# A four-layer image network: first loads on three queues, two output stages in source order, and first images read back in slices

## The chip, the cores and the metric

The kernel runs on one core of a Trainium2 chip. The metric is the device time of one execution in microseconds (us). All data are fp32. The engines are named as in the profile: PE is TensorE (matrix products and transposes), with PEld its weight loads; DVE is VectorE; ACT is ScalarE; POOL is GpSimd; SP is SyncE, which only issues DMAs. POOL and ACT can issue DMAs too.

## The reference

The input is x, 8 images of 56 x 56 positions with 192 channels. Four residual layers follow one another, each of the form x = x + f(GN(x)), where GN is a group normalisation over 32 groups of an image.

```
x = x + L0(_gn(x))    # silu projections, Toeplitz mixing along rows and columns, projection
x = x + L1(_gn(x))    # LN, shifted 7x7 window attention, 6 heads, projection
x = x + L2(_gn(x))    # 192 -> 384, 3x3 depthwise conv, four EMA scans, LN, 384 -> 192
x = x + L3(_gn(x))    # 7x7 depthwise conv + bias, LN, 192 -> 768, gelu, 768 -> 192, scale
return x
```

Layer 2's scans run s = 0.6 s + 0.4 x along rows and columns in both directions; their mean is added to the convolution's result before the layer norm (LN) over 384 channels. Layer 3's LN is over 192 channels.

## The kernel before

The layers run one after another over all 8 images, and most stages hand their results on through DRAM. On PE the stages lie at these times of the profiled execution: layer 0's projections 34 to 868 (L366), layer 0's mixing 875 to 2097; layer 1 2098 to 3558; layer 2's input projection (L790) 3613 to 3857; layer 2's mixing (L834, L858) 3885 to 4490; layer 2's output with layer 3's input (L911, L926, L973) 4546 to 5050; layer 3's convolution (L1009) 5072 to 5372; layer 3's output (L1065, L1087, L1098) 5411 to 6343.

**Order.** The program is written in Python with a tile framework. A scheduler decides the order of the instructions on every engine from dependences and priorities; tile pools with a number of buffers (`bufs`) make an instruction wait until the buffer that it needs is free, and tiles of different pools can lie on the same bytes, so a load into a new stage's tile can wait for the last reader of an old stage's tile. Each engine then works through its own list in order. DMAs are issued in the order of the list of the engine that issues them.

**Layer 1's start.** `layer1_load` (L595) loads an image rolled by 3 rows and columns, with 18 DMAs (`rolled`, L585), all on SP. `loaded` (L1165) loads images 0 and 1 before layer 0's mixing ends. The last store of layer 0's result is L476; `layer1_norm` begins at L600 with ACT's normalisation (L614) and PE's means (L621). At an image's end `rolled(x2[b], x[b], True)` stores it with 18 DMAs.

**Layer 2's input.** `layer2_in` (L765) loads an image on SP with two DMAs, normalises it on DVE (L778), clears borders on POOL (L776, L781), projects it on PE (L790), adds the bias on DVE and stores the tile pt to pd. The weights w_in and b_in are loaded by POOL's queue.

**Layer 2's mixing.** `layer2_mix` (L801) goes over 24 groups of 16 channels. `load` brings the band matrix wt and zc, the group's channels of all 8 images, 8 DMAs on SP. `front` (L828) convolves on PE (L834), copies loc and rows on ACT (L843), adds on POOL (L847), scans on DVE (L849 onwards); `back` (L854) multiplies by ema (L858) and copies to yc on ACT (L869); 8 DMAs per group store yc to md (L885). loc, rows and sums are one tile per group, of which `front` fills a quarter at a time.

**Layer 2's output and layer 3's input.** `layer2_load` (L888) loads one image of md as ml (112 partitions x 384 channels x 28 positions, 4.8 MB). `ln_pieces` (L187) takes bn_stats of the 28 pieces on DVE (L189); `ln_var` (L191) and `ln_rows` (L206) turn them into scale and shift with small DVE operations and one square root on ACT. An image has four groups k of up to four row pairs. `layer2_norm` (L893) scales ml into yt on DVE (L905) and ACT (L907), transposes it on PE (L911) and copies it to y with ACT (L912). `layer2_out` (L918) does the projection po on PE (L926) and adds it into x2o on DVE (L931), for three channel blocks j. After each block `between` (L1266) lets through an eighth of the next image's statistics and one or two steps of `layer3_in` (L935) of the image before: group statistics (L143 to L181), the normalised zp on POOL (L952), PE transposes zps (L973), copies zt (L960, L962) and the store zd (L986).

**Layer 3.** `convolve` (L988) goes over 12 groups of 16 channels like layer 2's mixing: wt (L997), zc (L1002), PE products cps (L1009), copies yc, 8 stores to yd per group (L1023). Then `layer3_load` (L1025) loads an image of yd as yl (2.75 MB), `layer3_norm` (L1035) adds the bias on POOL in four parts (L1043), takes 28 bn_stats (L189), computes rows, scales into yt on DVE (L1058), transposes on PE (L1065) and copies to y on ACT (L1076). `layer3_out` (L1078) does the two products ph (L1087) and po (L1098) with gelu into hid on ACT between (L1091), adds on DVE (L1105), and calls `between()` after every second ph block, twelve times an image, to let through one step of the next image's norm. yl has two buffers, and image b + 2 is loaded at the start of image b.

Of the kernel before, what the change touches and what calls it, by code (L numbers as in the profile page):

```python
# [29 lines left out]
HEADS, HD, WN = 6, 32, 49  # L30
C2 = 384
# [3 lines left out]
NPAIR = H // 2  # L35
# [41 lines left out]
def kernel(ctx: ExitStack, tc: tile.TileContext, a: dict, out: bass.AP):  # L77
# [113 lines left out]
    def ln_var(st, P, nch, pool):  # L191

        mean = pool.tile([P, NPAIR], F32, name="ln_mean")
        nc.vector.tensor_tensor(mean, st[:, :, 1], st[:, :, 4], ALU.add)
        d = pool.tile([P, NPAIR], F32, name="ln_d")
        nc.vector.tensor_tensor(d, st[:, :, 1], st[:, :, 4], ALU.subtract)
        nc.vector.tensor_tensor(d, d, d, ALU.mult)
        var = pool.tile([P, NPAIR], F32, name="ln_var")  # L200
        nc.vector.tensor_tensor(var, st[:, :, 2], st[:, :, 5], ALU.add)
        nc.vector.tensor_scalar(var, var, 1.0 / nch, None, ALU.mult)
        nc.vector.scalar_tensor_tensor(var, d, 0.25, var, ALU.mult, ALU.add)
        return mean, var

    def ln_rows(mean, var, P, eps, pool):  # L206

        rs = pool.tile([P, NPAIR], F32, name="ln_rs")
        nc.scalar.activation(rs, var, AF.Sqrt, bias=eps[0:P])
        nc.vector.reciprocal(rs, rs)  # L210
        mr = pool.tile([P, NPAIR], F32, name="ln_mr")
        nc.vector.scalar_tensor_tensor(mr, mean, -0.5, rs, ALU.mult, ALU.mult)
        return rs, mr

# [370 lines left out]
    def rolled(dram_image, tile_image, store):  # L585

        d = dram_image.rearrange("(j p) (h w) -> p j h w", p=64, w=W)
        for s, h0, h1, r0 in ((0, 0, 28, 3), (1, 0, 25, 31), (1, 25, 28, 0)):
            for w0, w1, c0 in ((0, 53, 3), (53, 56, 0)):
                for j in range(3):  # L590
                    sb = tile_image[64 * s:64 * s + 64, j, h0:h1, w0:w1]
                    dr = d[:, j, r0:r0 + h1 - h0, c0:c0 + w1 - w0]
                    nc.sync.dma_start(dr, sb) if store else nc.sync.dma_start(sb, dr)

    def layer1_load(b, pool):  # L595
        x = pool.tile([128, 3, H // 2, W], F32, name="x1")
        rolled(x1[b], x, False)
# [167 lines left out]
    def layer2_in(b, pool, xpool, psum, w_in, b_in):  # L765

# [5 lines left out]
        nc.sync.dma_start(x[0:64, :, 1:R2], src[:, :, 0:R2 - 1])  # L772
        nc.sync.dma_start(x[64:128, :, 0:R2 - 3], src[:, :, R2 - 1:H])
# [27 lines left out]
    def layer2_mix():  # L801
# [5 lines left out]
        with ExitStack() as st:  # L807
# [9 lines left out]
            def load(g):  # L817
# [5 lines left out]
                zc = pool.tile([128, nimg, CG2, P2], F32, name="zc2")  # L823
                for b in range(nimg):
                    nc.sync.dma_start(zc[:, b], pd[b][:, cs])
                return wt, zc

            def front(c4, wt, zc, loc, rows, sums):  # L828
# [9 lines left out]
                loc, rows, sums = (z[:, c4:c4 + 4].rearrange("p c z -> p (c z)") for z in (loc, rows, sums))  # L838
# [13 lines left out]
                )  # L852

            def back(c4, yc, loc, rows, sums):  # L854
                ps = psum.tile([2 * W, 2, 512], F32, name="mx2")
                for i in range(2):
                    for k, z in enumerate((loc, sums)):
                        nc.tensor.matmul(  # L858
                            ps[:, i, 0:2 * NG], ema[:, k],
                            z[:, c4 + 2 * i:c4 + 2 * i + 2].rearrange("p c z -> p (c z)"),  # L860
# [12 lines left out]
            for g in range(n + 1):  # L873
# [3 lines left out]
                following = [pool.tile([128, CG2, NG], F32, name=z) for z in ("loc", "rows", "sums")] if g < n else None  # L877
                for c4 in range(0, CG2, 4):
                    if g:
                        back(c4, yc, *now)  # L880
                    if g < n:
                        front(c4, *loaded[g], *following)
                if g:
                    for b in range(nimg):
                        nc.sync.dma_start(md[b][:, (g - 1) * CG2:g * CG2], yc[:, b])  # L885
                now = following

    def layer2_load(b, pool):  # L888
        ml = pool.tile([2 * W, C2, NPAIR], F32, name="ml")
        nc.sync.dma_start(ml, md[b])  # L890
        return ml, pool.tile([2 * W, NPAIR, 6], F32, name="ln_st")

    def layer2_norm(k, ml, rs, mr, pool, psum):  # L893


        n0 = 4 * k
        nn = min(4, PH - n0)
        nt = 2 * W * nn
        y = pool.tile([128, 3, 2, 8 * W], F32, name="y2")
        for s in range(2):  # L900
            yt = pool.tile([2 * W, 4, C2], F32, name="yt2")
            for i in range(nn):
                n = PH * s + n0 + i
                if i % 2 == 0:
                    nc.vector.tensor_scalar(yt[:, i], ml[:, :, n], rs[:, n:n + 1], mr[:, n:n + 1], ALU.mult, ALU.add)  # L905
                else:
                    nc.scalar.activation(yt[:, i], ml[:, :, n], AF.Identity, bias=mr[:, n:n + 1], scale=rs[:, n:n + 1])  # L907
            for m in range(3):
                tp = psum.tile([128, 4, 2 * W], F32, name="tp2")
                for i in range(nn):  # L910
                    nc.tensor.transpose(tp[:, i], yt[:, i, 128 * m:128 * m + 128], ident[0:2 * W, 0:2 * W])  # L911
                nc.scalar.activation(  # L912
                    y[:, m, s, 0:nt], tp[:, 0:nn].rearrange("p i n -> p (i n)"), AF.Identity,
                    bias=vec("be2", m), scale=vec("g2", m),
                )
        return y

    def layer2_out(k, y, x, psum, w_out, between):  # L918
# [3 lines left out]
        for j in range(3):  # L922
            ps = psum.tile([128, 512], F32, name="po2")
            for m in range(3):
                for s in range(2):
                    nc.tensor.matmul(  # L926
                        ps[64 * s:64 * s + 64, 0:nt], w_out[:, m, 64 * j:64 * j + 64], y[:, m, s, 0:nt],
                        start=(m == 0), stop=(m == 2),
                    )
# [489 lines left out]
```

## Time and profile before

| what | us |
|---|---|
| median of 3 runs | 6330.82 (6327.23 to 6345.44) |
| the profiled execution's own time | 6351.08 |
| its span, first to last instruction | 6349.2 |
| PE busy | 5569.1 (88% of the span) |
| DVE, ACT, POOL busy | 3439.3, 2239.7, 1302.1 |
| mean granted PE clock | 0.914 of full speed |

The profile is of one execution. Busy time of an engine says how long it had an instruction in work; a stage's bound shows in the stretch that holds it, in what ended the idle time of the engine that was idle. A row of waits reads: engine, operation and line that waited, after the arrow what ended the wait, then total us, times, and the longest. In a row of a stretch, behind its length, stand busy us and the number of instructions of each engine, the granted PE clock (which falls when PE is idle), the DMA engines' share and GB/s. In the chain each row has start, length and what ran. "issue" is time in which the profile shows no wait.

### The profile page before, as it was taken

How to read it: one execution, taken by the hardware profiler on the slowest of the kernel's cores; microseconds unless marked ns; L12 is line 12 of the kernel's file. 1: busy time of each engine (PE TensorE's matmuls, PEld its weight loads, DVE VectorE, ACT ScalarE, POOL GpSimd, SP SyncE). 2: the span in 40 equal slices, each digit the busy share in tenths (PEclk: the TensorE clock that was granted, in tenths of full speed). 3: DMA queues.
4: the chain of work that ended last, by engine and by line, in shares of the span. 5: the costliest groups of instructions: out<-in, count | busy, mean ns of one | idle time of the engine just before them, and what ended most of it. 6: DMA issues, size and time to landing. Idle time of an engine off the chain costs nothing. (4 is left out here: it accounts for less than half of the span.)

```text
span 6349.2 us, 126376 instructions
## 1 busy us (share of the span) xinstructions
PE 5569.1 (88%) x55636; PEld 3587.9 (57%) x55636; DVE 3439.3 (54%) x4752; ACT 2239.7 (35%) x2922; POOL 1302.1 (21%) x813
## 2 busy tenths in 40 slices
PE   6799989999999688888888598999588798789999
PEld 5677766666666345545445375777244498344444
DVE  5677765555665344444444486888688511532321
ACT  2334444443344233333332102555355300333333
POOL 1100034544444122122121102333110100110100
PEclk8899999999999888888888799999798799899999
DMA  6799886666665613444433675666667488121211
GB/s 166 185 221 210 188 262 263 260 253 240 240 252 194 88 33 55 60 58 63 55 48 44 103 266 208 224 228 233 153 203 208 170 305 305 64 67 56 70 54 27
DMA packets 1039131, 1013.10 MB, mean 160 GB/s; under 512 B 832104, under 2 KB 964372, under 8 KB 1011572
## 3 DMA queue, kind: packets, MB, share of 16 engines
q1 hardware_dynamic: 1028064, 954.17, 53.7%
q0 software_dynamic: 5648, 31.32, 1.5%
q10 hardware_dynamic: 4868, 19.52, 0.9%
q8 instruction: 437, 7.16, 0.5%
q14 instruction: 114, 0.93, 0.0%
HBM read 676.28 MB, written 345.08 MB: 161 GB/s over the span
## 5 line engine op out<-in xcount | busy, mean ns | idle before, releaser
L366 PE MATMUL qv<-w_qv_sb,xn 64*112 64x288 f32 x5376 | 722.2, 425 | 50.9 <-DVE act L372 47.6
L404 POOL COPY lc<-lt 128x896 f32<-128x896 f32 (+1 forms) x320 | 573.0, 1808 | 616.7 <-PE op L412 598.7
L366 PEld LDWEIGHTS qv<-w_qv_sb,xn 64*112 64x112 f32 x5376 | 535.5, 184 | 232.8 <-DVE act L372 64.7
L1087 PE MATMUL ph<-y,w_sb 64*128 64x392 f32 x2304 | 429.9, 511 | 49.1 <-ACT hid L1091 49.1
L373 ACT ACTIVATE act<-act 112x576 f32<-112x576 f32 x448 | 299.5, 682 | 461.7 <-DVE act L372 428.2
L1098 PE MATMUL po<-hid,w_sb 128*64 128x392 f32 x2304 | 395.1, 496 | 10.8 <-ACT hid L1091 10.8
L412 PEld LDWEIGHTS op<-rc,lc 128*56 128x56 f32 x9216 | 308.4, 136 | 127.6 <-issue 65.7
L412 PE MATMUL op<-rc,lc 128*56 128x56 f32 x9216 | 339.7, 222 | 46.0 <-POOL lc L404 24.2
L424 PE MATMUL pj<-xn,w_p_sb 64*128 64x392 f32 (+1 forms) x1920 | 373.0, 515 | 7.7 <-issue 4.7
L445 PE MATMUL y<-pp,w_o_sb 128*64 128x392 f32 (+1 forms) x1920 | 355.9, 503 | 20.4 <-DVE x L453 11.6
L372 DVE TENSOR_TENSOR act<-qv,b_qv 112x576 f32<-112x576 f32 x448 | 320.8, 751 | 86.1 <-PE qv L366 85.7
L1105 DVE TENSOR_TENSOR x<-x,z 128x392 f32<-128x392 f32 x96 | 55.8, 581 | 557.9 <-ACT z L1103 557.9
L1087 PEld LDWEIGHTS ph<-y,w_sb 64*128 64x128 f32 x2304 | 230.5, 194 | 224.1 <-ACT hid L1091 55.2
L404 ACT COPY rc<-rt 128x896 f32<-128x896 f32 (+1 forms) x160 | 256.9, 1606 | 230.7 <-PE op L412 216.0
L834 PE MATMUL cv<-zc,wt 128*128 128x224 f32 x1536 | 312.8, 355 | 27.9 <-DMA zc<-pd 27.9
L834 PEld LDWEIGHTS cv<-zc,wt 128*128 128x128 f32 x1536 | 290.5, 189 | 71.0 <-issue 54.9
L705 POOL TENSOR_TENSOR e<-e,mx 128x1176 f32<-128x1176 f32 x64 | 139.9, 2186 | 925.1 <-DVE mx L704 874.4
L655 PE MATMUL qk_ps<-xr,wg 64*96 64x392 f32 x1536 | 309.6, 511 | 14.9 <-ACT qk L661 13.3
L438 DVE TENSOR_TENSOR pp<-pp,ot 128x784 f32<-128x784 f32 (+1 forms) x160 | 154.6, 967 | 308.4 <-ACT pp L429 287.2
L1009 PE MATMUL cps<-zc,wt 128*128 128x224 f32 x1536 | 299.3, 356 | 23.1 <-DMA zc<-zd 22.5
L1009 PEld LDWEIGHTS cps<-zc,wt 128*128 128x128 f32 x1536 | 290.0, 189 | 32.5 <-issue 24.9
L847 POOL TENSOR_TENSOR rows<-rows,loc 128x896 f32<-128x896 f32 x96 | 228.1, 2377 | 390.2 <-ACT rows L843 262.8
(206 smaller groups left out, 9321.5 us busy)
## 6 DMA issues: line engine op xcount, KB each, us to landing
lt<-left SPq DMA_DIRECT2D x72, 1792.0 KB
rt<-right SPq DMA_DIRECT2D x72, 1792.0 KB
left<-qv SPq DMA_DIRECT2D x224, 252.0 KB
right<-qv SPq DMA_DIRECT2D x448, 126.0 KB
wt<-in_band_dram SPq DMA_DIRECT2D x24, 2048.0 KB
wt<-in_band_dram SPq DMA_DIRECT2D x12, 4096.0 KB
pd<-pt SPq DMA_DIRECT2D x8, 5568.0 KB
zc<-pd SPq DMA_DIRECT2D x192, 232.0 KB
```

The lines of the kernel that those rows point to most:

```text
L366: nc.tensor.matmul(ps[s][:, which, 0:D1 // 2], xn[64 * s:64 * s + 64, j, bass.ts(i, 2 * W)], w_qv[64 * s:64 * s + 64, j, which, ns], start ...
L372: nc.vector.tensor_tensor(act, ps[s][:, :, 0:D1 // 2], b_qv[:, :, ns], ALU.add)
L373: nc.scalar.activation(act, act, AF.Silu)
L404: copy(c[:, 0:nu], raw.rearrange("p (w u d) -> p u d w", u=nu, d=64 // nu)[:, :, d0:d0 + 8])
L412: nc.tensor.matmul(op[64 * u:64 * u + W, i, :], lc[:, u, i], rc[:, u, i], start=True, stop=True)
L424: nc.tensor.matmul(ps[0:M, s, 0:TT], w_p[64 * s:64 * s + 64, j, d0:d0 + M], xn[64 * s:64 * s + 64, j, ts], start=(j == 0), stop=(j == 2),)
L445: nc.tensor.matmul(y[64 * s:64 * s + 64], w_o[0:M, c, 64 * j:64 * j + 64], pp[0:M, s], start=(c == gated[0][0]), stop=(c == gated[-1][0]),)
L655: nc.tensor.matmul(ps[s], wg[64 * s:64 * s + 64, j, c0:c0 + HC], xw[64 * s:64 * s + 64, j, gs], start=(j == 0), stop=(j == 2),)
L834: nc.tensor.matmul(dst, wt[:, c4 + i, 128 * q:128 * q + 128], zc[:, :, c4 + i, q:q + NPAIR], start=(q == 0), stop=(q == 1),)
L1009: nc.tensor.matmul(dst.rearrange("p (b n) -> p b n", n=NPAIR), wt[:, c4 + i, q * OP:(q + 1) * OP], zc[:, :, c4 + i, q:q + NPAIR], start=(q ...
L1087: nc.tensor.matmul(ps[:, s, 0:TT], w0[64 * s:64 * s + 64, j, m * 128:(m + 1) * 128], y[64 * s:64 * s + 64, j, ts], start=(j == 0), stop=(j ...
L1098: nc.tensor.matmul(ps[64 * s:64 * s + 64], w1[:, m, 64 * j:64 * j + 64], hid[:, m, s], start=(m == 0), stop=(m == 5),)
```

## The change

- `rolled` and `layer1_load` take a list of queues. Image 0 of layer 1 is loaded over SP, POOL and ACT in turn; image 1's load is written after image 0's normalisation. One unused x1 tile shifts which buffer image 0 gets.
- `layer2_image` is split from `layer2_in`: image 0 of layer 2 is loaded by POOL's queue, later ones by SP, each written ahead of the image before it. w_in and b_in go to ACT's queue.
- In both convolutions, the first group's eight zc loads are spread over SP, POOL and ACT.
- In layer 2's mixing, loc, rows and sums become tiles of a quarter group with 6, 3 and 6 buffers. After each group's stores POOL reads image 0's slice of md back into ml. `convolve` does the same for yd, and POOL adds the bias to the slice.
- Image 0 of both output stages has its statistics, rows and scaling per group of rows (8 pieces at a time), not for the whole image at first.
- Layer 2's output with layer 3's input, and layer 3's output, are put under `manual_schedule` for PE, ACT and DVE: these three engines run the instructions of the stage in the order in which the source writes them. The source order is written so that yt of the next group comes before, and its transposes after, the projection of a block; the next image's statistics lie in blocks 3 to 8 of 12. The next x2o load is written at group 0, before at group 2.
- In layer 3's output the next image's norm is spread over more steps: bias at once, five of statistics, one of rows, then scaling a step ahead of its transposes.

```diff
-    def ln_var(st, P, nch, pool):
+    def ln_var(st, nch, pool):
...
+                    eng = queues[j % len(queues)]
...
-                    nc.sync.dma_start(dr, sb) if store else nc.sync.dma_start(sb, dr)
+                    eng.dma_start(dr, sb) if store else eng.dma_start(sb, dr)
...
-            x.extend(layer1_load(b, xpool) for b in range(min(2, nimg)))
+            for _ in range(-nimg % 3):
+                xpool.tile([128, 3, H // 2, W], F32, name="x1")
+            x.append(layer1_load(0, xpool, (nc.sync, nc.gpsimd, nc.scalar)))
...
         for _ in steps:
             pass
+        if nimg > 1:
+            x.append(layer1_load(1, xpool))
...
-        w_in = resident("w_in", nc.gpsimd, pool)
-        b_in = resident("b_in", nc.gpsimd, pool)
+        x = [layer2_image(0, xpool, nc.gpsimd)]
+        w_in = resident("w_in", nc.scalar, pool)
+        b_in = resident("b_in", nc.scalar, pool)
         for b in range(nimg):
-            layer2_in(b, pool, xpool, psum, w_in, b_in)
+            if b + 1 < nimg:
+                x.append(layer2_image(b + 1, xpool, nc.sync))
+            layer2_in(b, x[b], pool, psum, w_in, b_in)
...
+                queues = (nc.sync,) if g else (nc.sync, nc.gpsimd, nc.scalar)
                 for b in range(nimg):
-                    nc.sync.dma_start(zc[:, b], pd[b][:, cs])
+                    queues[b % len(queues)].dma_start(zc[:, b], pd[b][:, cs])
...
                     for b in range(nimg):
                         nc.sync.dma_start(md[b][:, (g - 1) * CG2:g * CG2], yc[:, b])
+                    nc.gpsimd.dma_start(first[:, (g - 1) * CG2:g * CG2], md[0][:, (g - 1) * CG2:g * CG2])
...
                 for b in range(nimg):
                     nc.sync.dma_start(yd[b][:, cs], yc[:, b])
+                nc.gpsimd.dma_start(first[:, cs], yd[0][:, cs])
+                add_bias(first[:, cs], dwb[:, cs])
...
+        st.enter_context(tc.manual_schedule(engines=IN_ORDER))
+        stat = lambda: pool.tile([2 * W, NPAIR, 6], F32, name="ln_st")
+        rows, own, steps, ready, y = [None], stat(), iter(()), None, None
...
+        def scaled(b, k, s):
+
+            if b:
+                return layer2_scaled(k, s, ml[b], *rows[0], 4 * k, pool)
+            if s == 0:
+                ns = slice(4 * k, min(4 * k + 4, PH))
+                ln_pieces(own, ml[0], [PH * r + n for r in range(2) for n in range(ns.start, ns.stop)])
+                rows[0] = ln_rows(*ln_var(in_halves(own)[:, :, ns], C2, pool), eps5, pool)
+            return layer2_scaled(k, s, ml[0], *rows[0], 0, pool)
...
+            for j in range(3):
+                if after and j < 2:
+                    if after[0] and after[1] == 0 and j == 0:
+                        rows[0] = ln_rows(*var_next, eps5, pool)
+                    following = scaled(*after, j)
+                if n >= 0:
+                    layer2_out(k, j, y, x[b], psum, w_out)
+                    i = 3 * k + j
+                    if b + 1 < nimg and 3 <= i < 9:
+                        ln_pieces(st_next, ml[b + 1], range(NPAIR * (i - 3) // 6, NPAIR * (i - 2) // 6))
+                    if b + 1 < nimg and i == 8:
+                        var_next = ln_var(in_halves(st_next), C2, pool)
+                    for _ in range(1 if i < 5 else 2):
+                        next(steps, None)
+                if after and j < 2:
+                    layer2_turned(after[1], j, following, y_next, psum)
...
-        steps = layer3_norm(yl[0], pool, psum, dwb)
-        y = [next(steps)]
-        for _ in steps:
-            pass
+        if nimg > 1:
+            yl.append(layer3_load(1, lpool))
+        st.enter_context(tc.manual_schedule(engines=IN_ORDER))
+        own, steps = layer3_norm(yl[0], pool, psum, None), iter(())
+        y = [next(own)]
+
+        next(own), next(own), next(own)
+
+        def between():
+            next(own, None)
+            next(steps, None)
```

## The prediction

> **What bounds the kernel now.** I read the shares of the page first, then busy time by stage, then the waits, then the chain of waits.
>
> ```profile
> span 6349.2 us, 126376 instructions
> ...
> PE 5569.1 (88%) x55636; PEld 3587.9 (57%) x55636; DVE 3439.3 (54%) x4752; ACT 2239.7 (35%) x2922; POOL 1302.1 (21%) x813
> ```
>
> TensorE is busy for 88% of the span, so a gain can only come from its idle time, or from an order that feeds it better. The view of stretches shows where it is idle; I cut at its own gaps.
>
> ```profile
> core 0: us, PE busy (x) PEld busy (x) DVE busy (x) ACT busy (x) POOL busy (x), PEclk, DMA share, GB/s
> 3557.00:3614.00 57.00, 1.35 (x6) 0.50 (x4) 5.51 (x9) 0.00 (x0) 4.16 (x10) 0.54 1.04 128
> 3856.00:3885.00 29.00, 1.11 (x3) 0.50 (x2) 1.09 (x2) 0.00 (x0) 3.97 (x3) 0.54 0.96 357
> 3884.00:4491.00 607.00, 598.07 (x2304) 422.61 (x2304) 525.56 (x288) 303.60 (x383) 228.14 (x96) 0.99 0.64 213
> 4490.00:4547.00 57.00, 1.16 (x5) 0.57 (x4) 24.60 (x40) 2.40 (x4) 6.04 (x6) 0.53 0.95 222
> 4546.00:5050.00 504.00, 426.70 (x2408) 226.04 (x2408) 387.38 (x699) 271.80 (x390) 47.99 (x68) 0.89 0.61 179
> 5049.00:5073.00 24.00, 1.52 (x6) 1.07 (x5) 1.24 (x2) 0.88 (x2) 0.00 (x0) 0.50 0.92 332
> 5371.00:5418.00 47.00, 5.52 (x20) 3.04 (x19) 28.45 (x55) 2.92 (x5) 20.56 (x8) 0.53 0.64 259
> 5418.00:6342.00 924.00, 864.18 (x4930) 431.21 (x4929) 268.40 (x554) 316.89 (x402) 63.83 (x24) 0.95 0.17 54
> ```
>
> Five stage boundaries leave TensorE empty: 57, 29, 57, 24 and 47 us; a sixth, into layer 1, is 22.01 us after 2105.04. At the first, second and fourth the DMA engines are over 90% busy throughout. At the third and fifth it is VectorE that works (24.60 and 28.45 us). The waits name the releasers:
>
> ```profile
> DVE yt L1058 <- PE tp L1065: 79.7, 22, 5.3
> PE tp L911 <- DVE yt L905: 57.8, 4, 55.8
> PE pin L790 <- POOL xn L781: 55.6, 1, 55.6
> DVE xn L778 <- DMA x<-x: 50.3, 1, 50.3
> PE ph L1087 <- ACT hid L1091: 49.1, 6, 10.0
> DVE x2o L931 <- PE po L926: 48.3, 54, 4.4
> ```
>
> The last two are steady losses, inside layer 3's and layer 2's output. The chain at the fifth boundary is a whole-image load, then POOL's bias, then the statistics of all 28 pieces:
>
> ```profile
> 5377.29 9.97 DMA yl<-yd
> ...
> 5387.51 2.54 POOL yl L1043
> ...
> 5390.07 11.63 DVE ln_st L189 x28
> ...
> 5401.73 1.28 DVE ln_mean L196
> 5403.00 2.63 DVE ln_d L198
> 5405.64 2.49 DVE ln_var L201
> ...
> 5410.16 4.31 DVE yt L1058 x9
> ```
>
> **What the Trainium skill says.** "DMA: Bandwidth & Descriptors", Issuing engines are not separate DMA queues: all issuing engines feed the same 16 DMA engines, so more queues save issue time only. The trace agrees: at the first two boundaries above the DMA share is 1.04 and 0.96 from one queue. The same page, Latency and other measured facts, gives about 2 us as a DMA's fixed cost; here a small store of the mixed output, issued at 4103.62, landed at about 4106.3. "GPSIMD Engine Reference", 1. Specifications: POOL shares its SBUF interfaces with VectorE and contends with VectorE instructions of two SBUF inputs. The trace agrees: the L196, L198, L201 row sums cost 1.28 to 2.63 us while POOL adds the bias, and 0.1 to 0.2 us at 5571, where POOL is idle.
>
> **The change, part by part.** Signs: minus is time gained.
>
> *Layer 1's first loads.* Before, SyncE issues 36 small-packet loads (both first images) from 2058.78 to 2112, and only then the last store of layer 0, which lands at 2126; ScalarE's first layer-1 operation starts at 2126.21, though image 0 has been in since 2086. What ends last is the store. In the changed program's order SyncE issues 6 loads of image 0, then 20 of later images, then the store: 26 ahead of it in place of 36, so 10 x about 1.5 us of issue, but those loads were limited by the DMA engines (22 us an image), and the 12 loads moved off still run. I take -4. ScalarE's six loads stand before the last five layer-0 activations, and could hold them: +14 at worst, -5 at best.
>
> *Layer 2's first image.* Image 0's load goes to POOL's queue, without the 18 last stores of layer 1 before it (3555.74 to 3594). But in the new order of VectorE, the first normalisation of image 1 stands before those of image 0, and image 1's load is on SyncE behind all 18 stores. That load is issued when image 0's was (3594.68), lands some 12 to 15 us later, and only then may image 0 be normalised. w_in and b_in move from POOL's queue to ScalarE's, where only layer 1's last copies stand before them: 0. I take +5; -25 if the order did not matter, +15 if the stores are slowed by the early loads.
>
> *Convolutions' first loads on three queues.* At 3856 some 9.7 MB pass at 357 GB/s, or 27 us: the gap is the DMA engines'. I take 0 (-3 to +3). At 5049 wt takes 15.06 us and is not moved; -2 (-4 to 0).
>
> *Layer 2's mix.* Same arithmetic in smaller tiles. New is POOL's read-back of an image slice, 24 times, which waits for the store of md and has POOL's next row add queued behind it, and VectorE's scan behind that. The store lands at 4106.3, the add began at 4106.33, the scan at 4110.8: hidden by about 2.4 us of slack. +2; if the cover is gone, 2 us x 24 = +48.
>
> *Start of layer 2's output.* Before: last yc 4491.6, 9.4 MB of loads to 4522, 28 statistics x 0.755 = 21.2, rows, yt: 4546.25. After: only the last slice is late (store about 2.5, read about 4 us: 4498), then 8 statistics (6.1), rows 1.7, yt 0.7: 4506, so -40. The other 20 statistics (15.1) and three more row computations (5) of image 0 now lie inside its own groups; VectorE is not free there for all of it, so image 0 takes about +12. Net -28 (-35 to -20).
>
> *Layer 2's output, steady.* TensorE has 426.7/8 = 53.3 us an image, VectorE 387.4/8 = 48.4; the time is (5026.8 - 4550.7)/8 = 59.5. In source order the 28 statistics lie in the 2nd and 3rd of the four groups only. There VectorE has 14 x 0.79 + yt 2.1 + x2o 1.9 + copies 2 = 17 us and, with the row sums and more of layer 3's steps, 19 to 20; TensorE's quarter is 13.3. Strictly bound per group: 13.3 + 17 + 19.5 + 13.3 = 63; with the two x2o buffers letting TensorE run ahead, 60. I take 61, +1.4 x 7 = +10 (-25 to +40). The next x2o load moves from the third group to the first on SyncE, ahead of zd stores; it waits for POOL's zp of the image before, done within the first slots: 0. The last image's group normalisation now stands after its last x2o in order: +7.
>
> *Start of layer 3's output.* From 5371.94 before to the first ph at 5418.09 was 46. After: store 2.5, slice 2.5, bias 0.9, 8 statistics x 0.415 = 3.3, rows 1.5 (POOL is idle, so no 2.6 us sums), 8 yt x 0.48 = 3.9, transposes 3: 5391. The 12 bias adds lie under the convolution (1.66 us of POOL in 300). Moved with them: w0's load, 1.2 MB, in POOL's order, stands behind the last add, where before it lay in the convolution at 5346; it shares the engines with 7.5 MB of SyncE loads, so it lands between 5384 and 5401, and I take 5391 too. Then image 0: before 5418.09 to 5562.86 = 144.8; after 105 (the undisturbed image below) + 5 own transposes + 10 for in-order stalls = 120. 190.9 becomes 139: -50 (-55 to -35).
>
> *Layer 3's output, steady.* The first ph of images 1 to 6 are at 5562.86, 5677.59, 5793.47, 5908.64, 6024.65, 6140.55: 115.5 each. Image 6, with no further load to wait for, takes 105.1. In the chain at 5546.13 a load, POOL, 28 statistics and a root on ScalarE stand before the first hid of the next image. After, that load is a whole image ahead, and the statistics and root are spread over steps in source order. 5 x 10 = -50 (-52 to -10).
>
> **Sum:** -4 + 5 + 0 - 2 + 2 - 28 + 10 + 7 - 50 - 50 = -110. Against the profiled execution's own 6351.1 (6349.2 and 1.9 around it) that is 6241; it ran 20 above the median of the runs shown, 6330.8, and on that footing the forecast is 6221.
>
> **Rivals.**
> (a) *Layer 3's images stay at 115.* If the wait of ph for hid comes back from ScalarE's own order (y copies and a table load ahead of the first hid; 1.28 us of it is seen at 5573.09), only the start gains: 6221 + 50 = 6271. For it: ScalarE is now bound to one order. Against: image 6 shows 105.1 with the same activations.
> (b) *The early loads do work.* If image 0's data alone releases layer 2, -30 against my +5, and the output of layer 2 falls to 55 an image, near TensorE's busy time, (55 - 59.5) x 7 = -31 against my +10: 6221 - 35 - 41 = 6145. Against: the VectorE order just told.
> (c) *Slower.* In layer 2's output, strict order makes TensorE and VectorE take turns: x2o waits behind statistics, po2's two buffers fill, transposes wait behind po. If in the two middle groups they add up (36.5 + 26.6) with 13.3 x 2 around, an image takes 90, +30 x 7 = +210 on the +10 taken: 6421. It decides from an extra 15 us an image (110/7.5). For it: VectorE waits 48.3 us for po already. Against: yt of the next group is asked for a slot ahead.
>
> **How the numbers follow.** Forecast 0.64 (6175 to 6260); (a) 0.15 (6250 to 6300); (b) 0.12 (6135 to 6175); (c) 0.05 (above 6350); several small losses together, about no gain, 0.04. The range 6150 to 6300 leaves out (c), the rest and about half of (b), some 0.15. A change within 0.3% (19 us) is about what a measurement of this kernel cannot tell from none. Faster by more: 0.92; within: 0.03; slower: 0.05.
>
> **What would show it.** The gap before L911 falls from 56 to about 16 us, that before the first ph from 46 to about 20; ph's waits for hid fall from 49 us to under 15; image period in layer 3 about 105. The gaps near 3557, 3857 and 5050 stay. The forecast is wrong if layer 2's output needs more than 70 us an image, if row adds wait for read-backs, or if the first hid still waits for a root.

## The result

The changed kernel takes 6306.43 us (median of 6 runs, 6295.86 to 6315.91) against 6329.52 for the kernel before (6 runs beside it, 6316.35 to 6345.44): a ratio of 0.996, 95% interval 0.9946 to 0.9974. It is faster by 0.4%, some 23 us; 110 were forecast. Its profiled execution took 6315.91 us, 35.2 less than that of before, and the sums below are of these two.

The page of the changed kernel (shares of the span; then two rows of the costliest groups, with what ended the idle time before them at the end):

```profile
span 6314.0 us, 126563 instructions
...
PE 5528.6 (88%) x55636; PEld 3582.6 (57%) x55636; DVE 3442.3 (55%) x4800; ACT 2253.9 (36%) x2932; POOL 1337.6 (21%) x869
...
L1121 PE MATMUL ph<-y,w_sb 64*128 64x392 f32 x2304 | 398.3, 498 | 6.4 <-ACT hid L1125 6.4
...
L799 PE MATMUL pin<-w_in_sb,xn 64*128 64x384 f32 x1392 | 236.4, 489 | 67.9 <-POOL xn L790 67.9
```

The share of TensorE is as before. The wait of ph for hid is nearly gone (49.1 us before, now 6.4), and the wait before layer 2's first product has grown from 55.6 to 67.9. The view of stretches, cut at the changed kernel's own gaps:

```profile
core 0: us, PE busy (x) PEld busy (x) DVE busy (x) ACT busy (x) POOL busy (x), PEclk, DMA share, GB/s
...
3557.00:3626.00 69.00, 1.14 (x6) 0.46 (x5) 8.33 (x12) 1.28 (x1) 2.24 (x4) 0.53 0.86 119
3867.00:3897.00 30.00, 1.33 (x5) 0.71 (x4) 1.16 (x2) 0.00 (x0) 5.40 (x6) 0.53 0.97 360
3896.00:4512.00 616.00, 602.39 (x2304) 423.76 (x2304) 525.79 (x288) 303.25 (x383) 235.87 (x119) 0.99 0.66 216
4511.00:4531.00 20.00, 0.89 (x4) 0.16 (x2) 8.71 (x19) 1.73 (x3) 6.58 (x7) 0.58 0.85 215
4530.00:5098.00 568.00, 420.25 (x2408) 231.05 (x2408) 404.81 (x745) 281.00 (x393) 54.09 (x72) 0.85 0.57 166
5097.00:5119.00 22.00, 0.81 (x5) 0.57 (x4) 1.21 (x2) 0.88 (x2) 0.00 (x0) 0.52 1.03 376
5420.00:5451.00 31.00, 4.82 (x18) 2.89 (x18) 21.09 (x45) 2.73 (x6) 12.86 (x8) 0.59 0.91 368
5450.00:6308.00 858.00, 826.62 (x4935) 417.60 (x4933) 287.37 (x590) 323.59 (x411) 64.50 (x24) 0.99 0.18 59
```

The third gap fell from 57 to 20 us and the last from 47 to 31, as meant. But the stage between them, 4530 to 5098, is 568 us where it was 504. TensorE's work in it is about the same (427 us before, now 420); VectorE's grew from 387 to 405, since the later statistics of image 0 now lie inside the stage. Out of 568 us they are idle for about 150 and 160. The next table cuts the profiled executions at the first and last product of each stage (us):

| part | before | after | change | forecast |
|---|---|---|---|---|
| to layer 1's first product | 2127.1 | 2126.2 | -0.9 | -4 |
| layer 1 | 1430.6 | 1431.7 | +1.0 | 0 |
| gap to layer 2 | 55.7 | 67.9 | +12.2 | +5 |
| layer 2's input | 243.3 | 242.0 | -1.3 | 0 |
| gap, mixing's first loads | 27.9 | 28.7 | +0.8 | 0 |
| layer 2's mixing | 605.9 | 615.5 | +9.6 | +2 |
| gap to layer 2's output | 55.8 | 19.1 | -36.7 | -40 |
| layer 2's output, layer 3's input | 503.3 | 566.3 | +63.1 | +29 |
| gap, convolution's first loads | 22.5 | 21.2 | -1.3 | -2 |
| convolution | 299.9 | 302.1 | +2.2 | 0 |
| gap to, and layer 3's output | 970.5 | 886.7 | -83.8 | -100 |

In words: 120 us of gain came in at the two places where it was meant to. Of these, 63 were given back in layer 2's output, 12 at layer 2's first image and 10 in the mixing.

### The profile page after: what moved, and what is told of

It reads as the page before. It is cut to its first block, busy times and chain, and to the rows that moved or that the text cites. A ratio compares the mean times of both kernels' runs of the same rounds, so it can differ in the third digit from the quotient of the medians.

```text
span 6314.0 us, 126563 instructions
## 1 busy us (share of the span) xinstructions
PE 5528.6 (88%) x55636; PEld 3582.6 (57%) x55636; DVE 3442.3 (55%) x4800; ACT 2253.9 (36%) x2932; POOL 1337.6 (21%) x869
## 5 line engine op out<-in xcount | busy, mean ns | idle before, releaser
L1121 PE MATMUL ph<-y,w_sb 64*128 64x392 f32 x2304 | 398.3, 498 | 6.4 <-ACT hid L1125 6.4
L450 PE MATMUL y<-pp,w_o_sb 128*64 128x392 f32 (+1 forms) x1920 | 358.0, 505 | 22.5 <-DVE pp L443 8.7
L1139 DVE TENSOR_TENSOR x<-x,z 128x392 f32<-128x392 f32 x96 | 72.0, 750 | 521.1 <-ACT z L1137 521.1
L844 PE MATMUL cv<-zc,wt 128*128 128x224 f32 x1536 | 312.2, 355 | 28.7 <-DMA zc<-pd 28.7
L661 PE MATMUL qk_ps<-xr,wg 64*96 64x392 f32 x1536 | 309.0, 511 | 15.1 <-ACT qk L667 13.6
L799 PE MATMUL pin<-w_in_sb,xn 64*128 64x384 f32 x1392 | 236.4, 489 | 67.9 <-POOL xn L790 67.9
```

The lines of the kernel that those rows point to most:

```text
L450: nc.tensor.matmul(y[64 * s:64 * s + 64], w_o[0:M, c, 64 * j:64 * j + 64], pp[0:M, s], start=(c == gated[0][0]), stop=(c == gated[-1][0]),)
L661: nc.tensor.matmul(ps[s], wg[64 * s:64 * s + 64, j, c0:c0 + HC], xw[64 * s:64 * s + 64, j, gs], start=(j == 0), stop=(j == 2),)
L844: nc.tensor.matmul(dst, wt[:, c4 + i, 128 * q:128 * q + 128], zc[:, :, c4 + i, q:q + NPAIR], start=(q == 0), stop=(q == 1),)
L1121: nc.tensor.matmul(ps[:, s, 0:TT], w0[64 * s:64 * s + 64, j, m * 128:(m + 1) * 128], y[64 * s:64 * s + 64, j, ts], start=(j == 0), stop=(j ...
```

## The experiments

All are of the changed kernel with edits; an edit acts in its own stage and is read there. Experiments 1 to 7 were run once each, 8 and 9 several times. Layer 1, which no edit touches after its first product, took 1415 to 1435 us in these profiles, so single totals are good to some 10 us and the stages are the better measure. A stage isn't exact either: layer 2's output took 522.8 us in experiment 1 and 516.3 in experiment 8, which are alike in it.

### 1. Layer 2's output back to the scheduler; read-back by SyncE

```diff
-        st.enter_context(tc.manual_schedule(engines=IN_ORDER))
         stat = lambda: pool.tile([2 * W, NPAIR, 6], F32, name="ln_st")
...
-                    nc.gpsimd.dma_start(first[:, (g - 1) * CG2:g * CG2], md[0][...])
+                    nc.sync.dma_start(first[:, (g - 1) * CG2:g * CG2], md[0][...])
```

> The changed kernel, with two edits in stages apart. (1) The output of layer 2 is given back to the scheduler: the source-order region is not entered there, all else in the stage stays. In the changed kernel the stage, first transpose to last transpose of layer 3's input, takes 566 us, 68.2 an image, with TensorE and VectorE both about 51 us busy an image. Theory A (the one fixed order makes the engines take turns): the period falls to 63 or less, the stage to 500-530. Rival B (the new placing of work, such as statistics in a few blocks or smaller pieces, costs the time whatever the order): it stays at 560-575. (2) The read-back of image 0's slice in layer 2's mixing is issued by SyncE in place of POOL. Theory C (POOL's row adds stand behind the read-back's wait): the mixing, 615.5 us, falls to 606-610. Rival D (something else in the smaller tiles): it stays at 614-617.

6249.55 us. The stage fell from 566.3 to 522.8, within A's range; images 1 to 6 took 64.9 us each on average in place of 68.2, where A had said 63 or less. B falls. The mixing took 607.7, as C said; with the read-back on SyncE it was 607.7, 609.4 and 608.8 in three kernels, on POOL 609.8 to 615.5 in seven (mean 612.3). By the means, POOL's wait costs about 4 of the 9.6 us; the ranges all but touch, and the rest is not settled.

### 2. Statistics over nine blocks; y ahead of the next statistics

```diff
-                    if b + 1 < nimg and 3 <= i < 9:
-                        ln_pieces(st_next, ml[b + 1], range(NPAIR * (i - 3) // 6, NPAIR * (i - 2) // 6))
+                    if b + 1 < nimg and i < 9:
+                        ln_pieces(st_next, ml[b + 1], range(NPAIR * i // 9, NPAIR * (i + 1) // 9))
```

In layer 3's first image, the transposes and y of row group i0 - 4 are moved ahead of the statistics, rows and scaling of group i0.

> The changed kernel, with two edits in stages apart. (1) The next image's statistics in layer 2's output lie in the first nine of twelve blocks, about 3 each, and not in six with 4 or 5 each; order stays that of the source. Theory A1 (VectorE's runs of 5 statistics hold up what stands behind them): the period falls from 68.2 to about 63-65. Rival A2 (the length of the run doesn't matter, the chain of handovers does): 67.5-69. (2) In layer 3's first image the transposes and y of a row group are put before the next group's statistics, rows and root. Theory: the first ph is held by w0's load alone, which lands at 5448.7 just as y does, so the gap from the last convolution product to the first ph stays at 29-30 us. Rival: the root in ScalarE's order was what held y and w0 was in before: it falls to 20-23.

6360.17 us, slower than the kernel before. The stage grew to 625.1, an image to 75.3. Both theories failed. The first group of an image, 14.0 us in the changed kernel, took 21.1: 7.1 us more, as much as the whole image grew. That group already holds the group statistics of layer 3's input (gh_st), which start a chain from VectorE to TensorE and back. From this kernel's timeline, the first group of image 3:

```profile
4769.35 2.40 DVE L190 BATCH_NORM_STATS2 ln_st<-ml 112x6 f32<-112x384 f32 x3
4771.66 2.90 DVE L144 BATCH_NORM_STATS2 gh_st<-x2o 128x6 f32<-128x392 f32 x6
...
4776.14 2.38 DVE L190 BATCH_NORM_STATS2 ln_st<-ml 112x6 f32<-112x384 f32 x3
```

Each of the group's three blocks puts about 2.4 us of ml's statistics into VectorE's order, ahead of the group statistics in the first two, and together they are the 7.1 us. The second edit: the gap from the last convolution product to the first ph fell from 29.9 to 22.4, so the rival was right: the next group's statistics and root, ahead in the order, had held y.

### 3. Copies before statistics; w0 early

```diff
+                    for _ in range(1 if i < 5 else 2):
+                        next(steps, None)
                     if b + 1 < nimg and 3 <= i < 9:
...
-                    for _ in range(1 if i < 5 else 2):
-                        next(steps, None)
...
+        w0 = resident("w0", nc.gpsimd, lpool)
+        w1 = resident("w1", nc.gpsimd, lpool)
         convolve(yl[0], dwb)
```

and the second edit of experiment 2.

> The changed kernel, with two edits in stages apart. (1) In a block of layer 2's output, the steps of layer 3's input (group statistics, copies zt) stand before the next image's statistics and not after them. Theory A3 (ScalarE's small zt copy waits for VectorE's zt copy behind 5 statistics, and ScalarE's y behind that, and TensorE's transposes behind y: 4.8 + 4.6 us an image seen): the period falls from 68.2 to 59-63. Rival A2 (the wait only moves, to x2o or yt): 67 or more. (2) In layer 3's first image, w0 and w1 are loaded before the convolution into memory of their own, and the y of a row group comes before the next group's statistics. Both candidates for the late first ph are gone: the gap from the last convolution product to the first ph falls from 29.9 to 18-21 us. Rival: yt or the read-back itself is the limit: 25 or more.

6308.11 us. The stage took 562.7, an image 66.8: the wait that this edit takes away was only moved (rival A2, or nearly: 67 was its bound). The gap to the first ph was 20.9, as forecast, and 1.5 less than in experiment 2, without w0's early load.

### 4. First loads

```diff
-            x.append(layer1_load(0, xpool, (nc.sync, nc.gpsimd, nc.scalar)))
+            x.append(layer1_load(0, xpool))
...
-        x = [layer2_image(0, xpool, nc.gpsimd)]
+        x = [layer2_image(0, xpool, nc.scalar)]
```

with image 0's borders cleared by ScalarE (a product with zero) in place of POOL, and w0, w1 early.

> The changed kernel, with three edits at stage boundaries. (1) Layer 1's image 0 is loaded by SyncE alone. Theory: ScalarE's DMA issues had held its last layer-0 activations by 11 and 6 us; layer 0's last product comes back from 2110.6 to 2096-2098, and the first layer-1 product from 2126 to 2114-2127, since the last store still decides. Rival: it was not ScalarE's queue: 2108 or later. (2) Layer 2's image 0 is loaded on ScalarE's queue and its borders are cleared by ScalarE, so that nothing of image 0 stands behind image 1 in any engine's order. Theory: the gap before layer 2's first product falls from 67.9 to 15-25 us. Rival: the stores of layer 1 or the weights hold it anyway: 50 or more. (3) w0 and w1 are loaded before the convolution. If w0 alone held the first ph, the gap falls from 29.9 to about 20; if the root in ScalarE's order did, it stays at 28-30.

6287.83 us. (1) Layer 0's last product came at 2090.2 and layer 1's first at 2107.0, both earlier than the theory said; the latter is 19 us earlier than in the changed kernel and 20 earlier than before it. So the spread of image 0's load over three queues had cost about as much as the rest of the change gains there. What held layer 0 is in the timeline of the changed kernel (start, length, engine, line; in brackets the idle time before):

```profile
2053.95 0.53 ACT L529 COPY o<-op 56x448 f32<-56x448 f32 x1 [0.70 <-PE op L417]
2055.04 10.44 ACTq L599 DMA_DIRECT2D x<-x  x3
2065.58 0.91 ACT L434 ACTIVATE pp<-pj,vecs_sb 128x784 f32<-128x784 f32 x1 [11.10 <-issue]
2065.61 6.02 ACTq L599 DMA_DIRECT2D x<-x  x1
```

ScalarE spends 10.44 us on issuing three small-packet loads (most packets have 212 or 12 bytes), and the activation behind them waits 11.10 us. (2) The gap to layer 2 was 55.4: the rival's side. On ScalarE's queue image 0's load was issued only after SyncE's last store of layer 1:

```profile
3535.50 35.73 SPq L599 DMA_DIRECT2D x<-x  x18
...
3571.39 0.69 ACTq L777 DMA_DIRECT2D x<-x  x1
```

Before it, ScalarE's queue waits for six of the eight completion counters that these 18 stores use; the wait for two of them lasts from 3538.72 to 3571.28. (3) The gap to the first ph stayed at 29.1 with w0 early and nothing else changed there: w0 was not what held it.

### 5. VectorE free; images 0 and 1 of layer 2 on POOL's queue

```diff
-        st.enter_context(tc.manual_schedule(engines=IN_ORDER))
+        st.enter_context(tc.manual_schedule(engines=IN_ORDER - {mybir.EngineType.DVE}))
         stat = lambda: pool.tile([2 * W, NPAIR, 6], F32, name="ln_st")
...
-                x.append(layer2_image(b + 1, xpool, nc.sync))
+                x.append(layer2_image(b + 1, xpool, nc.sync if b else nc.gpsimd))
```

with the read-back by SyncE, layer 1's image 0 by SyncE alone, image 0's borders by ScalarE.

> The changed kernel with edits in stages apart. (1) Layer 2's output: only TensorE and ScalarE keep the source's order, VectorE is given back to the scheduler. With all three in order an image takes 68.2 us, with none 62 to 63. Theory V (VectorE's fixed order is what couples the engines): 64 or less, the stage 525-540. Rival P (TensorE's and ScalarE's order does it): 67 or more, the stage 560-570. (2) The slice read-back of the mixing by SyncE again: 606-609 as in the first experiment. (3) Layer 1's image 0 by SyncE alone, as before: first layer-1 product near 2107. (4) Layer 2's images 0 and 1 both on POOL's queue, image 0's borders cleared by ScalarE, so that nothing of image 0 stands behind image 1 and image 0's load does not wait for one of the stores' completion counters, as it did on ScalarE's queue (32.6 us). The gap before layer 2's first product falls from 55 to 15-22 us; rival: the small-packet stores slow the load or the weights, 40 or more.

6233.48 us. The stage took 511.4, below V's range, and an image 61.7: P falls. The mixing took 609.4 and layer 1's first product came at 2110.0. VectorE's wait for po fell by more than half, first line the changed kernel, second this one:

```profile
DVE x2o L943 <- PE po L938: 121.8, 54, 5.3
...
DVE x2o L946 <- PE po L941: 53.9, 38, 3.8
```

(4) The gap before layer 2 fell to 18.0 us, but the wait came back inside the stage. From the timeline of this kernel:

```profile
3554.77 13.30 PE L802 MATMUL pin<-w_in_sb,xn 64*128 64x384 f32 x72 [17.98 <-ACT xn L794]
...
3560.37 1.54 DVE L810 TENSOR_TENSOR pt<-pin,b_in_sb 128x768 f32<-128x768 f32 x1 [0.39 <-PE pin L802]
3606.29 3.29 DVE L787 TENSOR_SCALAR xn<-x,scsh 128x1680 f32<-128x1680 f32 x3 [44.37 <-DMA x<-x]
...
3611.07 4.21 PE L802 MATMUL pin<-w_in_sb,xn 64*128 64x384 f32 x12 [43.01 <-DVE pt L810]
```

After two of image 0's sums, VectorE's next instruction is image 1's normalisation. That image's load is issued at 3586.10, after layer 1's last stores, and ends at 3606; TensorE's buffers fill and it stands 43 us. Gap and stage together: 305.2 us, against 309.9 changed and 298.9 before.

### 6. Statistics in three blocks; layer 3's output back to the scheduler

```diff
-                    if b + 1 < nimg and 3 <= i < 9:
-                        ln_pieces(st_next, ml[b + 1], range(NPAIR * (i - 3) // 6, NPAIR * (i - 2) // 6))
+                    if b + 1 < nimg and 6 <= i < 9:
+                        ln_pieces(st_next, ml[b + 1], range(NPAIR * (i - 6) // 3, NPAIR * (i - 5) // 3))
...
-        st.enter_context(tc.manual_schedule(engines=IN_ORDER))
         own, steps = layer3_norm(yl[0], pool, psum, None), iter(())
```

> The changed kernel with two edits in stages apart. (1) Layer 2's output in source order, the next image's 28 statistics in three blocks (the third group) with 9 or 10 each. Six blocks gave 68.2 us an image, nine gave about 75. Theory H (each block that holds statistics costs a handover of about 2.3 us; the line through both points meets 54.6 at none): about 61-62. Rival L (a long run on VectorE starves TensorE for its length): 67 or more. (2) Layer 3's output is given back to the scheduler, with the rest of its changes (loads an image ahead, finer steps, first image in parts) kept. Theory: the loads an image ahead and the finer steps make the gain there, and the stage stays at 865-885 us from 871.5. Rival: the order itself made it: 900 or more (931 in the kernel before).

6433.05 us. An image took 78.8 us: the line through two points was wrong, and rival L's figure came in. Its reason, that a run of 9 or 10 statistics starves TensorE, fits: the third and fourth groups grew most (26.3 and 22.9 us, table below). The second edit shows what the source order does for layer 3: the stage, from its first transpose to its last product, went from 871.5 to 932.2 us, though the place of the loads, the finer steps and the first image in parts were kept.

```profile
5492.00:6424.00 932.00, 869.90 (x4944) 434.17 (x4944) 283.00 (x607) 321.00 (x410) 72.69 (x28) 0.95 0.18 60
```

This is the level of the kernel before (931.1). The rival was right: without the order nothing of that gain is left. Whether the order would make it without the finer steps was not tested.

### 7. Only VectorE in source order

```diff
-        st.enter_context(tc.manual_schedule(engines=IN_ORDER))
+        st.enter_context(tc.manual_schedule(engines={mybir.EngineType.DVE}))
         stat = lambda: pool.tile([2 * W, NPAIR, 6], F32, name="ln_st")
```

with the boundaries of experiment 5 and y first as in experiment 2.

> The changed kernel with edits in stages apart. (1) Layer 2's output: only VectorE keeps the source's order, TensorE and ScalarE are the scheduler's. Theory V (VectorE's fixed order couples the engines): 66-69 us an image, the stage 550-570. Rival P: 64 or less, the stage 525-540. (2) y before the next statistics in layer 3's first image, as before: stage 866. (3) Boundaries as in the fifth experiment: first layer-1 product near 2107, gap before layer 2's first product 15-22.

6230.94 us; the stage 520.8, an image 62.3. So theory V falls, as P did in experiment 5: VectorE alone in order costs nothing that shows, nor do TensorE and ScalarE alone, while all three together cost 3 to 7 us an image. The other parts came as forecast (layer 1's first product at 2106.2, the gap before layer 2 18.5 us, layer 3's stage 866.1). Time of each of the four groups, from the starts of po, mean of images 1 to 6 (us):

| kernel | k = 0 | 1 | 2 | 3 | image | stage |
|---|---|---|---|---|---|---|
| before | 23.4 | 12.8 | 16.2 | 10.4 | 62.8 | 503.3 |
| changed | 14.0 | 13.9 | 21.7 | 18.6 | 68.2 | 566.3 |
| 1, scheduler | 23.3 | 13.8 | 15.1 | 12.7 | 64.9 | 522.8 |
| 3, copies first | 14.0 | 15.7 | 18.0 | 19.0 | 66.8 | 562.7 |
| 5, VectorE free | 12.9 | 15.9 | 19.6 | 13.4 | 61.7 | 511.4 |
| 7, only VectorE in order | 12.9 | 16.7 | 12.9 | 19.8 | 62.3 | 520.8 |
| 2, nine blocks | 21.1 | 16.4 | 19.6 | 18.3 | 75.3 | 625.1 |
| 6, three blocks | 14.0 | 15.6 | 26.3 | 22.9 | 78.8 | 637.7 |

### 8. The order undone alone, timed

The first edit of experiment 1 alone.

> The changed kernel with one edit alone: layer 2's output is given back to the scheduler. Theory A (the source order of three engines in this stage took back most of the gain): the stage is 515-530 us as in the first experiment (522.8; 566.3 in the changed kernel) and the time falls by 40-50 from the changed kernel's 6306, to 6255-6268, some 1.1% below the kernel before. Rival: part of the first experiment's 66 us came from elsewhere and the stage's 43 is not worth 43 in the time: 6275 or more.

6258.75 us, ratio to the kernel before 0.9886 (0.9865 to 0.9907); the stage 516.3, an image 63.1. That is 48 us under the changed kernel by the medians, 50 by the stage: theory A holds. Of the 63 us that the stage had lost, 50 belong to the order here and 43 in experiment 1; the rest stays without it, most of it in image 0 (59.5 us; 55.4 before) and in the last image (51.1; 43.7).

### 9. A version to beat both

Experiments 5 and 2's second edit together, and the normalisation of images 1 and 2 on ScalarE:

```diff
+            if b in (1, 2):
+                nc.scalar.activation(
+                    xn[:, j, :, 0:W], x[:, j], AF.Identity, bias=sh[:, j:j + 1], scale=sc[:, j:j + 1]
+                )
+                continue
```

> A version meant to beat both. The changed kernel with: VectorE free in layer 2's output (stage about 511 us), layer 1's image 0 by SyncE alone (first layer-1 product near 2108), the slice read-back of the mixing by SyncE, y ahead of the next statistics in layer 3's first image (stage 866), and layer 2's images 0 and 1 on POOL's queue with image 0's borders and the normalisation of images 1 and 2 on ScalarE. In the fifth experiment the gap before layer 2's first product fell from 68 to 18, but VectorE then stood 43 us at image 1's normalisation with image 0's sums behind it, so gap and stage together stayed at 305 us (310 in the changed kernel). Theory: with that normalisation off VectorE, image 0's products run under the wait and gap and stage together fall to 272-285; the time is 6195-6215. Rival (image 1 comes so late that TensorE waits for it anyway): 292 or more, 6220-6235.

6211.41 us (5 runs, 6206.98 to 6213.13), within the theory's range; ratio to the kernel before 0.9807 (0.9789 to 0.9824). Gap and stage of layer 2's input together came to 288.7, between theory and rival. The last line is TensorE's longest wait in that stage:

```profile
3533.00:3552.00 19.00, 0.26 (x1) 0.00 (x0) 5.13 (x8) 0.36 (x2) 0.00 (x0) 0.59 1.10 218
3552.00:3822.00 270.00, 243.06 (x1420) 165.06 (x1420) 192.50 (x141) 12.33 (x9) 15.99 (x36) 0.93 0.77 217
4480.00:4992.00 512.00, 413.50 (x2408) 226.36 (x2408) 398.55 (x737) 278.82 (x392) 49.33 (x72) 0.89 0.63 182
...
PE pin L807 <- POOL xn L797: 25.9, 1, 25.9
```

The stage holds 243 us of TensorE's work in 270; 26 of the rest is the wait for image 1, whose load still stands behind layer 1's last stores.

## Why the prediction was wrong, step by step

**The step that failed: "with the two x2o buffers letting TensorE run ahead, 60. I take 61".** It failed twice over. The time that it was set against, 59.5, is the mean of eight images of which the last has no next image's statistics; images 1 to 6 alone took 62.8 before. And the estimate took each group to be as long as its busier engine needs. Images 1 to 6 took 68.2 each, all within 0.3 us, with TensorE and VectorE busy for only 51 us each. In one fixed order on three engines such a group is as long as its chain of handovers, in which one engine waits for another in turn. The timeline of the changed kernel, at the end of the third group of image 1, shows one such chain:

```profile
4660.58 3.91 DVE L190 BATCH_NORM_STATS2 ln_st<-ml 112x6 f32<-112x384 f32 x5
...
4664.52 0.21 DVE L199 TENSOR_TENSOR ln_mean<-ln_st 112x28 f32<-112x28 f32 x1
...
4665.53 1.17 DVE L973 COPY zt<-zps 128x512 f32<-128x512 f32 x2
4666.71 1.57 PEld L984 LDWEIGHTS zps<-ident,zp 128*128 128x128 f32 x8 [4.98 <-issue]
4666.74 0.27 ACT L971 COPY zt<-zps 64x64 f32<-64x64 f32 x1 [5.23 <-DVE zt L973]
4666.85 0.32 ACT L212 ACTIVATE ln_rs<-ln_var,eps 112x28 f32<-112x28 f32 x1
```

Five statistics and the row sums stand on VectorE before the copy zt that frees TensorE's zps buffer; ScalarE waits 5.23 us for the same copy, with the root and the y of the next group behind it. TensorE's loads wait 4.98. Taking this one wait away (experiment 3) gave 1.4 us an image: other handovers took most of its place, and which ones was not followed further. Freeing VectorE, or TensorE and ScalarE, from the order (5, 7) gave 6. Against the 29 us forecast, the stage lost 63: 32 in images 1 to 6 (6 x 5.4), 16 in image 0 (55.4 to 71.8; 12 forecast), 10 in the last (7 forecast), 4 at the start. This is rival (c)'s mechanism, engines taking turns, at a sixth of its price. Without the source order in this stage the change is worth 1.1% (experiment 8); with it, 0.4%. By the profiles the forecast missed by 75 us in all: 34 here, 16 in layer 3's output, the other 25 in small pieces.

**Layer 3's output, start and steady: right in kind, too high by 16.** Images 1 to 5 went from 115.5 to 106.5 (-45; -50 forecast). The reason given was half right. The load is no further ahead than it was: image 3's was issued at 5546.13 before and at 5549.66 in the changed kernel, each time over 230 us ahead of that image's first ph. Experiment 6 shows that the order is what counts, and the traces show how. ScalarE's root for image 3, first line before, second in the changed kernel:

```profile
5572.33 0.32 ACT L209 ACTIVATE ln_rs<-ln_var,eps 128x28 f32<-128x28 f32 x1 [7.11 <-DVE ln_var L203]
...
5732.87 0.32 ACT L212 ACTIVATE ln_rs<-ln_var,eps 128x28 f32<-128x28 f32 x1
```

Before, it stood ahead of the first hid of image 1, two images early, and waited there for statistics; now it comes in the middle of image 2 and waits for nothing. The wait that went had cost twice. One image, first line before, second in the changed kernel:

```profile
5677.59:5793.47 115.88, 107.19 (x619) 53.59 (x618) 36.94 (x81) 40.12 (x52) 12.37 (x5) 0.96 0.20 66
...
5678.27:5784.81 106.54, 102.94 (x620) 52.06 (x618) 37.94 (x76) 40.08 (x51) 10.68 (x4) 1.00 0.22 72
```

Of the 9.3 us, 5.1 are idle time of TensorE and 4.3 its busy time, for the same products. In the kernel before, TensorE stood 8.69 us for hid until 5691.07; the granted clock was 0.50 from 5684.6 to 5694.8, and the ten products ph from 5691 to 5694 took 889 ns each in the mean, against 498 for all ph of the changed kernel. The forecast's 105, read off image 6, held both parts.

The first ph came 29.9 us after the last convolution product, not 19. I named w0's load as the thing that might hold it; experiment 4 shows that it wasn't (29.1 with w0 early), experiment 2 that the order ahead of y, with the second group's root in it, was (22.4). From the timeline of the changed kernel:

```profile
5437.91 10.34 POOL L1046 TENSOR_TENSOR yl<-yl,dwb 128x1344 f32<-128x1344 f32 x4 [7.72 <-DMA yl<-yd]
5443.22 2.54 DVE L201 TENSOR_TENSOR ln_d<-ln_d 128x8 f32<-128x8 f32 x1
5445.88 2.40 DVE L203 TENSOR_SCALAR ln_var<-ln_var 128x8 f32<-128x8 f32 x1
5448.51 0.30 ACT L212 ACTIVATE ln_rs<-ln_var,eps 128x8 f32<-128x8 f32 x1 [14.67 <-DVE ln_var L204]
5448.72 1.32 ACT L1109 ACTIVATE y<-tp,vecs_sb 128x448 f32<-128x448 f32 x2
```

POOL, said to be idle there, adds image 1's bias, and two of the small operations on VectorE that fall within it take 2.54 and 2.40 us in place of 0.17; that such sums grow beside POOL had been seen before, but POOL's next image was forgotten. ScalarE's root waits for them, and y for the first group, ready since 5440, waits behind the root.

**Start of layer 2's output: right.** -36.7 for -40.

**Layer 2's first image: right in its reason, low in its size.** +12.2 for +5: image 1's normalisation ahead of image 0's, on VectorE, held TensorE until 3625.68. The size was missed because the stores ahead of image 1's load took longer, first lines before, last lines the changed kernel:

```profile
3555.74 38.40 SPq L593 DMA_DIRECT2D x<-x  x18
3594.68 0.59 SPq L772 DMA_DIRECT2D x<-x  x1
...
3555.89 46.53 SPq L599 DMA_DIRECT2D x<-x  x18
3605.64 0.59 SPq L777 DMA_DIRECT2D x<-x  x1
```

Image 1's load was issued at 3605.64, 11 us later than the forecast took. Issuing the 18 stores took 45.8 to 46.7 us in all nine kernels that load image 0 over POOL's queue beside them, and 35.73 in experiment 4, which loads it after them. This is the case named for +15, stores slowed by the early load. That undoing the order is worth little as long as image 1's load stands behind the stores was not foreseen (experiments 5 and 9).

**Layer 1's first loads: near the number by luck, with two errors that cancel.** Layer 0's last product came 14 us later than before (2110.6 for 2096.7), the worst end of the bound, and 20 later than in experiment 4, where ScalarE issues none of these loads. On the other side, layer 0's last store, which layer 1 waits for, was issued 16 us after the last product before (2112.69) and 1 us after it in the changed kernel (2111.21), since SyncE has 26 loads ahead of it and not 36. The forecast had worked out these 10 x 1.5 us of issue, and then took 4.

**Mixing: low by 8**, of which about 4 is the read-back (experiment 1); the others stay open. The store that the forecast timed landed at 4105.84 rather than 4106.3, which changes nothing in it.

**The convolutions' first loads:** as forecast, nothing: with three queues the DMA share in the two gaps is 0.97 and 1.03, and they last 28.7 and 21.2 us for 27.9 and 22.5. The 1.04 and 0.96 that the forecast put down to one queue hold 0.09 and 0.02 of POOL's queue.

## What to carry to other kernels

In this kernel a source order on three engines at once paid where one engine is the bound and the others wait for it (layer 3's output, -60 us), and cost where two engines have nearly equal work with handovers between them (51 and 51 us busy in 68): there, leaving one side free took the cost away. These are one stage each; try both ways. Before trusting the busier engine of a group as its time, write down the order on each engine and follow who waits behind whom. When a first load is brought forward, look for the instruction of the second load's data that stands in the same queues, since the wait may only move. Issue no long list of small-packet DMAs from an engine with work behind them: here it held layer 0 for 14 to 20 us. And when a mean over images is the yardstick, leave out those that do less work.

## What was not expected of the hardware

ScalarE was held for 10.44 us by the issue of three small-packet loads. Sums of 8 columns on VectorE with two inputs took 0.17 us alone and one of them 2.54 beside a POOL addition; an operation with one input tensor took 2.40 there. Products of TensorE right after a wait of 8.69 us took 889 ns in place of 498, at a granted clock of 0.50. The issue of 18 small-packet stores by SyncE took 46 us with one more load beside them and 36 without.
